# The first norm of a four-layer kernel: two batches ahead of the attention, six inside it

## The chip, the core and the metric

The kernel runs on one core of a Trainium2 chip. The core has five engines with queues of their own: TensorE (PE in the profile; its weight loads are PEld), VectorE (DVE), ScalarE (ACT), GpSimd (POOL) and SyncE (SP), which here only issues DMA transfers. SBUF is the working memory with 128 partitions, PSUM the eight banks into which PE writes. The metric is the device time of one execution in microseconds (us): the median of three runs.

## The reference

Four layers work on x of 8 batches x 512 tokens x 128 features, in float32. Each one is a norm, an attention-like part s, a feed-forward part g, and a gated sum:

```python
xn = _layernorm(x, axis=-1)
s = _L0_attn_ref(xn, ...)          # 16 heads of 8, sliding window of 64
g = _silu(_L0_ffn_ref(xn, ...))    # six 128x128 weights in 4 bits with scales and low-rank parts
x = x + s * g
# layer 1: a recurrence over time (s) and experts, two of eight per token (g)
# layer 2: windowed and latent attention (s), a complex product (g)
# layer 3: complex attention with decays per head (s), soft experts (g)
```

The norm takes each token's mean and variance over the 128 features: `(x - m) / sqrt(v + eps)`. The change touches this first norm, layer 0's attention, and work that prepares weights for later layers:

- decoding in layer 0: `w = q / 7.5 - 1`, times a scale per group of 16;
- mixing in layer 1: the key, value and receptance weights are scaled per input channel by the time mix, and by one minus it; the output weights are halved;
- scalars in layer 3: softplus, sigmoid, and a chain of products and reciprocals on 16 heads.

## The kernel before

x lies in SBUF with features on the partitions and tokens along the free axis. A batch is 512 tokens, and the norm's blocks are 512 tokens too (NTB is 8), so a block of the norm is a batch.

**Who orders the instructions.** Instructions issued through `in_order` (line 74) keep the order in which they are written, on each engine. All of them appear under line 83 in the profile, so they are told apart by the names of their tiles. Other instructions are placed by a scheduler, each as early as its operands and its buffers let it. A pool of buffers hands one out again when its last reader is done; the profile shows that as a wait on that reader.

**The start** (`network`, line 2757). SP loads x in eight parts, then the weights of layers 2 and 1 (in the constructors of `L2Consts` and `L1Consts`), then the attention's `a0_w` and `a0_b`, then layer 0's 4-bit weights (`l0_load`). The norm runs over all eight blocks. Then `l0_decode`, `l2.fill` and `l1.fill` are written (masks and counters on POOL; two large loads m1_w13 and m1_w2 from ACT's queue; the mixing on ACT), and then the attention. `l3_scalars` is written after layer 0, but it is left to the scheduler, and the profile shows it between 34 and 43 us.

**The norm** (`layer_norm`, line 117). Four steps per block: `centre` (four PE products with the centring matrix into ps_c), `spread` (ACT squares, DVE sums to var, POOL takes the power -0.5 to rstd), `scale` (DVE multiplies ps_c by rstd into row), `turn` and `keep` (four PE transposes into ps_t, ACT copies to xn). It has all eight banks of PSUM; the attention's pools open when it ends.

**The attention** (`l0_attention`, line 225). It works in 64 units u, eight per batch; a unit is 128 tokens and eight heads. Three pools of PSUM: scores (two tiles of two banks), one bank of weighted sums, and three banks `p_t` for everything else. The loop writes, for unit u:

- `turned(u)`: eight PE transposes of the exponentials, in two halves (tp), each copied by ACT (pt);
- in even units `norm(u - 1)`: DVE takes the reciprocal (rec) and the product (o);
- `scores(u + 3)`: four PE products (sc), DVE adds the mask (e) and takes the maxima (mx), POOL subtracts them;
- in even units `out_rows`: one PE transpose (tpo), ACT adds a bias (ot);
- ACT's exponential of unit u + 2;
- `weigh(u)`: 16 small PE products (av; 32 records in the profile);
- in a batch's second unit `finish`: the output projection of the batch before (ps_o on PE, s on DVE);
- one step of `project`, for the next batch: first the key projection ps_k with the first two of four masked copies kb (DVE, then ACT), next the other two kb (DVE, then ACT), then the queries (ps_q), then the values in two parts (ps_v).

So the bank of ps_k is held from the end of a batch's first unit to the end of its second. From the fifth batch on, `l0_low_rank` adds a step in each batch's seventh unit, on the decoded weights. Behind the attention comes `l0_ffn`, which needs the decoded weights; layer 1 needs the mixing, and layer 3 the scalars.

Of the kernel before, what the change touches and what calls it, by code (L numbers as in the profile page):

```python
# [9 lines left out]
F32 = mybir.dt.float32  # L10
# [6 lines left out]
P = 128  # L17
# [10 lines left out]
class Net:  # L28
# [88 lines left out]
    def layer_norm(self, x, xn, gamma=None, beta=None, banks=(5, 3), free=False):  # L117
# [7 lines left out]
        with tc.tile_pool(name="ln_s", bufs=3) as sp, tc.tile_pool(  # L125
# [41 lines left out]
            for t in range(NTB + 3):  # L167
                if t < NTB:
                    centre(t)
                    spread(t)  # L170
                if 2 <= t < NTB + 2:
                    scale(t - 2)
                if t >= 3:
                    turn(t - 3)
                    keep(t - 3)
# [49 lines left out]
def l0_attention(net, xn, s_out, p0, w, bias):  # L225
# [6 lines left out]
    with ExitStack() as st:  # L232
# [148 lines left out]
        act.activation(e[1], e[1], AF.Exp)  # L381
        todo = iter(())
        for u in range(N + 2):
            if u < N and u % U == 0 and u // U + 1 < B:
                todo = project(u // U + 1)
# [20 lines left out]
            if u > 4 * U and u % U == 6:  # L406
                next(low, None)

# [290 lines left out]
class L1Consts:  # L699
    E = 8  # L700

    def __init__(self, net, st):
        nc, tc, E = net.nc, net.tc, self.E
        self.net = net
        self.p1 = p1 = st.enter_context(tc.tile_pool(name="a1_c", bufs=1))
# [7 lines left out]
    def fill(self):  # L713
        net, nc, p1, E = self.net, self.net.nc, self.p1, self.E
        act = net.in_order(nc.scalar)
        self.w13 = net.load(p1, "m1_w13", act)
        self.w2 = net.load(p1, "m1_w2", act)

        w, par = self.w, self.par
        self.td = td = p1.tile([P, 1], F32, tag="td", name="td")  # L720
        act.activation(td, par[:, 0:1], AF.Exp)
        act.activation(td, td, AF.Copy, scale=-1.0)
        self.tf = par[:, 1:2]
        self.wm = wm = p1.tile([P, 3, 2, P], F32, tag="wm", name="wm")
        self.rest = rest = p1.tile([P, 3], F32, tag="rest", name="rest")
        act.activation(rest, par[:, 2:5], AF.Identity, scale=-1.0, bias=net.ones[:, 0:1])
        for i in range(3):
            act.activation(wm[:, i, 0, :], w[:, i, :], AF.Copy, scale=par[:, 2 + i : 3 + i])
            act.activation(wm[:, i, 1, :], w[:, i, :], AF.Copy, scale=rest[:, i : i + 1])
        act.activation(w[:, 3, :], w[:, 3, :], AF.Copy, scale=0.5)  # L730
# [22 lines left out]
        nc.gpsimd.memset(self.keep[:, :, 0:1], 0.0)  # L753

# [554 lines left out]
class L2Consts:  # L1309
# [4 lines left out]
    def __init__(self, net, st):  # L1314
# [5 lines left out]
        self.p1 = p1 = st.enter_context(tc.tile_pool(name="a2_c", bufs=1))  # L1320
# [1315 lines left out]
class Prepared:  # L2636
# [29 lines left out]
    def l0_decode(self):  # L2666
        nc, wt, qw, sc = self.net.nc, self.f0_wt, self.qw, self.sc
        nc.vector.tensor_copy(wt, qw)
        nc.vector.tensor_scalar(wt, wt, 1.0 / 7.5, -1.0, ALU.mult, ALU.add)
        nc.vector.tensor_tensor(wt, wt, sc, ALU.mult)  # L2670
# [34 lines left out]
    def l3_scalars(self):  # L2705
# [9 lines left out]
        nc.vector.scalar_tensor_tensor(sp, raw, -1.0, raw, ALU.mult, ALU.min)  # L2715
        nc.scalar.activation(sp, sp, AF.Exp)
        nc.scalar.activation(sp, sp, AF.Ln, bias=net.ones[:, 0:1])
        nc.vector.scalar_tensor_tensor(sp, raw, 0.0, sp, ALU.max, ALU.add)
        sig2, eta2, gam2, nu = (sp[:, i, :] for i in range(4))

# [4 lines left out]
        nc.scalar.activation(mu, par[:, 0, :], AF.Exp, scale=-1.0)  # L2725
        nc.vector.tensor_scalar(mu, mu, 1.0, None, ALU.add)
        nc.vector.reciprocal(mu, mu)
        nc.vector.tensor_scalar(mu, mu, 1e-4, None, ALU.add)
        nc.vector.tensor_scalar(nmu, mu, -1.0, None, ALU.mult)

        nc.vector.tensor_scalar(v_e2, nmu, 2.0, None, ALU.mult)
        nc.vector.reciprocal(v_e2, v_e2)
# [132 lines left out]
```

## Time and profile before

| What | us |
|---|---|
| Median of three runs | 2364.72 (2363.43 to 2366.03) |
| The profiled execution's own time | 2379.87 |
| Its span, first to last instruction | 2378.2 |
| First scores of the attention | 43.24 |
| First transposes of the attention | 50.97 |
| Key projections (ps_k) of the next batches | 56.59, 101.52, 133.36, 165.21, 197.05, 229.61, 262.38 |

Over the whole span PE is busy 93%, DVE 84%, ACT 78%, POOL 66%. The profile cuts the span into 40 slices of 59.5 us; the first five hold all that the change moves. A digit is the busy share in tenths, PEclk is the clock granted to TensorE in tenths of full speed:

```profile
PE   5999998989976999878999999999999999999888
DVE  4577778875675999759999999999999999999656
ACT  3566655555533899947999999999999999999865
POOL 4344435254264788656688888888788878887545
PEclk7799988999997999988999999999999999999999
```

A line of a timeline gives start and length in us, engine, line, operation, output and inputs, the number of instructions, and in brackets the idle time before it with what ended it. A line of a window gives the stretch, its length, and for each engine its busy time with the number of instructions in brackets; then the granted clock as a fraction of full speed, the DMA engines' share and GB/s. PE's busy time is that of records whose ends are modelled; a PE that is busy at clock 0.5 does half the work. A float32 product appears as two records, a transpose as one.

### The profile page before, as it was taken

Reading aid. Unit: us, or ns where it says so; the run is one execution under the profiler, and the core shown is the slowest. Engines: PE = TensorE matmul, PEld = TensorE weight load, DVE = VectorE, ACT = ScalarE, POOL = GpSimd, SP = SyncE. Lnnn points to the kernel's source line nnn. Section 1 sums busy time; section 2 is a strip of 40 time slices with the busy share of each in tenths; the row PEclk is TensorE's granted clock in tenths of the full one; section 3 lists DMA queues with packets and bytes.
Section 4 is the critical chain, followed back from the end, with each engine's and each line's share of the span. In section 5 each row is a group of like instructions: output and inputs, shape, how many; then the busy total and the mean of one; then the engine's idle time right before and its main releaser. Section 6 shows DMA issues by size and latency. Waiting matters only on the chain.

```text
span 2378.2 us, 48959 instructions
## 1 busy us (share of the span) xinstructions
PE 2203.3 (93%) x17762; PEld 1535.1 (65%) x17762; DVE 1996.1 (84%) x3579; ACT 1854.9 (78%) x3906; POOL 1575.0 (66%) x1414
## 2 busy tenths in 40 slices
PE   5999998989976999878999999999999999999888
PEld 4666676656533666645767777777777777777676
DVE  4577778875675999759999999999999999999656
ACT  3566655555533899947999999999999999999865
POOL 4344435254264788656688888888788878887545
PEclk7799988999997999988999999999999999999999
DMA  4000001012210000043334344443444344433100
GB/s 141 2 2 2 2 1 36 9 50 66 46 43 20 3 16 16 29 119 98 99 98 116 103 105 103 104 104 103 109 106 109 91 109 114 107 97 85 41 1 37
DMA packets 91617, 156.94 MB, mean 66 GB/s; under 512 B 20144, under 2 KB 44464, under 8 KB 91120
## 3 DMA queue, kind: packets, MB, share of 16 engines
q1 hardware_dynamic: 86736, 140.95, 22.7%
q0 software_dynamic: 4352, 8.92, 1.6%
q10 hardware_dynamic: 288, 3.93, 0.4%
q8 instruction: 142, 2.33, 0.4%
q14 instruction: 99, 0.81, 0.1%
HBM read 30.52 MB, written 12.06 MB: 18 GB/s over the span
## 4 chain that ended last, share of the span: by engine, by line
PE 58%; DVE 28%; issue 4%; POOL 4%; ACT 4%; DMA 1%; SPq 1%; another core or an unknown queue 0%; DVEq 0%; ACTq 0%; POOLq 0%
PE sc L83 11%; DVE sc L83 8%; DVE y L83 6%; DVE r L83 6%; PE ps_av L83 6%; PE tp L83 5%; PE ps_u L83 5%; PE ps_kq L83 5%; PE ps_n L83 3%; PE av L83 3%; PE ps_ab L83 3%; PE ps_v L83 2%; DVE mx L83 2%; DVE e L83 2%; PE ps_y L83 1%
## 5 line engine op out<-in xcount | busy, mean ns | idle before, releaser
L83 POOL TENSOR_TENSOR ek<-E,kn 128x512 f32<-128x512 f32 (+3 forms) x512 | 433.5, 868 | 209.6 <-DMA kn<-nr 205.9
L83 POOL TENSOR_TENSOR e<-e,mx 128x1024 f32<-128x1024 f32 x112 | 212.1, 1899 | 190.1 <-DVE mx L83 93.6
L83 PE MATMUL sc<-r 128*128 128x512 f32 (+3 forms) x1024 | 311.9, 448 | 26.9 <-DVE y L83 24.0
L83 POOL TENSOR_TENSOR r<-r,rs 128x1024 f32<-128x1024 f32 x128 | 303.8, 2373 | 22.9 <-DMA rs<-r 17.7
L83 PE MATMUL ps_av<-u,at 128*128 128x128 f32 x2560 | 308.1, 276 | 0.8 <-ACT o L83 0.8
L83 PEld LDWEIGHTS ps_av<-u,at 128*128 128x128 f32 x2560 | 297.4, 193 | 1.1 <-ACT o L83 1.1
L83 ACT ACTIVATE y<-y,mn 128x384 f32<-128x384 f32 (+3 forms) x512 | 288.4, 569 | 4.0 <-DVE mn L83 3.2
L83 PEld LDWEIGHTS sc<-r 128*128 128x128 f32 x1024 | 166.2, 192 | 192.6 <-issue 125.6
L83 DVE SCALAR_TENSOR_TENSOR y<-sc,qn,V 128x512 f32<-128x512 f32 (+3 forms) x512 | 246.6, 544 | 9.1 <-DVE sc L83 0.5
L83 DVE CUSTOM_DVE_ANT_0 y<-y,ps_g,ncs 128x384 f32<-128x384 f32 (+3 forms) x512 | 253.1, 540 | 0.0
L83 PEld LDWEIGHTS tp<-ident,y 128*128 128x128 f32 x1280 | 161.4, 141 | 115.3 <-issue 48.7
L83 ACT ACT_TABLE_LOAD x179 | 229.7, 1283 | 3.9 <-PEq L2854 0.8
L83 PE MATMUL tp<-ident,y 128*128 128x128 f32 x1280 | 203.7, 274 | 3.4 <-ACT o L83 1.4
L83 ACT COPY at<-tp 128x512 f32<-128x512 f32 (+1 forms) x384 | 195.1, 508 | 7.6 <-PE tp L83 4.6
L83 DVE SCALAR_TENSOR_TENSOR sc<-sc,ek 128x1280 f32<-128x1280 f32 x128 | 189.6, 1482 | 8.9 <-issue 3.8
L83 DVE TENSOR_TENSOR sc<-sc,EF 128x1280 f32<-128x1280 f32 x128 | 191.9, 1499 | 4.4
L83 POOL TENSOR_TENSOR s<-s,o 128x512 f32<-128x512 f32 x120 | 153.7, 1281 | 32.5 <-ACT o L83 32.5
L83 ACT ACTIVATE y<-y 128x1280 f32<-128x1280 f32 x128 | 163.4, 1277 | 6.5 <-DVE y L83 5.8
L83 DVE TENSOR_TENSOR r<-sn,ps_kq 128x1024 f32<-128x1024 f32 x128 | 155.1, 1212 | 10.3 <-ACT sq L83 5.4
L83 ACT ACTIVATE sq<-ps_kq 128x1024 f32<-128x1024 f32 x128 | 131.5, 1027 | 33.6 <-PE ps_kq L83 33.6
L83 DVE TENSOR_TENSOR r<-ct,ps_kq 128x1024 f32<-128x1024 f32 x128 | 155.0, 1211 | 0.0
L83 ACT ACTIVATE e<-e 128x1024 f32<-128x1024 f32 x112 | 117.3, 1061 | 40.5 <-POOL e L83 40.0
(459 smaller groups left out, 5035.7 us busy)
## 6 DMA issues: line engine op xcount, KB each, us to landing
rs<-r SPq DMA_DIRECT2D x256, 256.0 KB
kn<-nr SPq DMA_DIRECT2D x512, 64.0 KB
yrows<-yy SPq DMA_DIRECT2D x36, 128.0 KB
ct<-trig SPq DMA_DIRECT2D x16, 256.0 KB
EF<-E SPq DMA_DIRECT2D x16, 256.0 KB
EF<-E SPq DMA_DIRECT2D x16, 192.0 KB
m_w<-m_w ACTq DMA_DIRECT2D x1, 2560.0 KB
x<-x SPq DMA_DIRECT2D x8, 256.0 KB
```

Source lines behind the costliest of these rows:

```text
L83: ins = op(*args, **kwargs)
```

## The change

`layer_norm` gets a number of blocks, and `network` asks for two. The other six blocks become steps in the attention's loop: a generator `centred(b)` for the block two batches ahead. It is advanced at the top of a batch's second to seventh unit, ahead of the unit's transposes: the products and a copy to SBUF by ACT (lc), the square on ACT, the sum on DVE, the power and the product on POOL, an empty step, then the transposes into a `p_t` bank and the copy to xn.

A second chain, `early()`, is advanced at the top of the fourth, sixth and eighth unit from the second batch on: decoding (three steps, its last product on POOL instead of DVE), mixing (six steps on ACT), and the scalars of layer 3 (on DVE and ACT, in written order now).

The loads of layers 2 and 1 move out of the constructors into `load()`, called behind `l0_load`; so the attention's weights are the first load after x. The two large loads of `l1.fill` move from ACT's queue to SP's.

```diff
-    def layer_norm(self, x, xn, gamma=None, beta=None, banks=(5, 3), free=False):
+    def layer_norm(self, x, xn, gamma=None, beta=None, banks=(5, 3), free=False, n=NTB):
...
-            for t in range(NTB + 3):
-                if t < NTB:
+            for t in range(n + 3):
+                if t < n:
...
-def l0_attention(net, xn, s_out, p0, w, bias):
+def l0_attention(net, x, xn, s_out, p0, w, bias, l1):
...
+        def centred(b):
+            ps = p_t.tile([P, 4, P], F32, tag="t", name="ps_c")
+            for k in range(4):
+                pe.matmul(
+                    ps[:, k, :], lhsT=x[:, ts(4 * b + k, P)], rhs=net.cmat,
+                    start=True, stop=True,
+                )
+            c = p2.tile([P, 4, P], F32, tag="lc", name="lc")
+            act.copy(c, ps)
+            yield
+            sq = p2.tile([P, 4, P], F32, tag="sq", name="sq")
+            act.activation(sq, c, AF.Square, scale=net.inv_root)
+            var = p2.tile([P, 4], F32, tag="var", name="var")
+            std = p2.tile([P, 4], F32, tag="rstd", name="rstd")
+            yield
+            dve.tensor_reduce(var, sq, AX.X, ALU.add)
+            dve.tensor_scalar(var, var, EPS, None, ALU.add)
+            yield
+            pool.tensor_tensor(std, var, net.neg_half.to_broadcast([P, 4]), ALU.pow)
+            pool.tensor_tensor(c, c, std.unsqueeze(2).to_broadcast([P, 4, P]), ALU.mult)
+            yield
+            yield
+            ps = p_t.tile([P, 4, P], F32, tag="t", name="ps_t")
+            for k in range(4):
+                pe.transpose(ps[:, k, :], c[:, k, :], net.ident)
+            act.copy(xn[:, ts(b, S)], ps.rearrange("p k q -> p (k q)"))
+            yield
+
+        def early():
+            yield from net.prep.l0_decode(dve, pool)
+            yield from l1.mixing(act)
+            yield from net.prep.l3_scalars(dve, act)
+
+        rest = early()
         todo = iter(())
+        norms = iter(())
         for u in range(N + 2):
+            if u % U == 0 and u // U + 2 < B:
+                norms = centred(u // U + 2)
+            if 0 < u % U < 7:
+                next(norms, None)
+            if u >= U and u % U in (3, 5, 7):
+                next(rest, None)
...
-        act = net.in_order(nc.scalar)
-        self.w13 = net.load(p1, "m1_w13", act)
-        self.w2 = net.load(p1, "m1_w2", act)
+        self.w13 = net.load(p1, "m1_w13")
+        self.w2 = net.load(p1, "m1_w2")
...
+    def mixing(self, act):
+        act.activation(td, par[:, 0:1], AF.Exp)
+        act.activation(td, td, AF.Copy, scale=-1.0)
+        yield
+        act.activation(rest, par[:, 2:5], AF.Identity, scale=-1.0, bias=net.ones[:, 0:1])
+        yield
+        for i in range(3):
+            act.activation(wm[:, i, 0, :], w[:, i, :], AF.Copy, scale=par[:, 2 + i : 3 + i])
+            act.activation(wm[:, i, 1, :], w[:, i, :], AF.Copy, scale=rest[:, i : i + 1])
+            yield
+        act.activation(w[:, 3, :], w[:, 3, :], AF.Copy, scale=0.5)
+        yield
...
-        nc.vector.tensor_tensor(wt, wt, sc, ALU.mult)
+        yield
+        pool.tensor_tensor(wt, wt, sc, ALU.mult)
+        yield
...
-    def l3_scalars(self):
+    def l3_scalars(self, dve, act):
...
+        yield
+        dve.scalar_tensor_tensor(sp, raw, -1.0, raw, ALU.mult, ALU.min)
+        act.activation(sp, sp, AF.Exp)
+        act.activation(mu, par[:, 0, :], AF.Exp, scale=-1.0)
+        yield
+        act.activation(sp, sp, AF.Ln, bias=net.ones[:, 0:1])
+        yield
...
-            net.layer_norm(x, xn)
-            prep.l0_decode()
+            l2.load()
+            l1.load()
+            net.layer_norm(x, xn, n=2)
             l2.fill()
             l1.fill()
-            l0_attention(net, xn, s, p0, w0, b0)
+            l0_attention(net, x, xn, s, p0, w0, b0, l1)
             l0_ffn(net, x, xn, s, l1)
-        prep.l3_scalars()
```

## The prediction

> **What bounds the kernel now.** I read the page first (the chain that ended last, then the 40 slices), then stage windows of the first 395 us, then the timeline of 0 to 60 us and of one batch in the middle of the attention. Everything that the change touches lies before 310 us of the 2378.2 us span, so only that stretch is priced. Its windows (time stretch, length, then busy time and count of PE, PEld, DVE, ACT and POOL, granted clock, DMA share, GB/s):
>
> ```profile
> 0.00:43.24 43.24, 23.21 (x115) 19.36 (x115) 18.57 (x54) 18.85 (x36) 22.07 (x73) 0.79 0.60 194
> 56.59:101.52 44.93, 44.43 (x409) 29.02 (x407) 22.60 (x27) 20.08 (x32) 15.08 (x8) 0.63 0.00 1
> 133.36:165.21 31.85, 30.51 (x409) 19.97 (x409) 23.55 (x28) 20.79 (x33) 15.17 (x9) 1.00 0.01 2
> ```
>
> The reader is to see three stages. Up to 43.24, where the first scores start, no engine is busy much over half of the time: this is a chain of waits. From there a batch of the attention is the stretch from one key projection (ps_k) to the next. In steady state it takes 31.85 us with PE busy 30.51 of it: PE is the bound, and DVE (23.55), ACT (20.79) and POOL (15.17) have room. The first such batch holds the same 409 PE records and takes 44.93 us at a mean clock of 0.63, which is 13.1 us more. Finer windows put the clock at 0.50 without a break from 48.6 to 89.6, though PE is busy nearly all of that time.
>
> The start, from the timeline (start, length, engine, operation):
>
> ```profile
> 10.88 4.00 POOL L83 TENSOR_TENSOR rstd<-var,neg_half 128x4 f32<-128x4 f32 x4
> 30.55 2.07 PE L83 MATMUL ps_k<-xn,a_w 128*128 128x512 f32 x2 [0.67 <-ACT xn L83]
> 36.99 0.76 ACT L83 ACTIVATE kb<-ps_k,kbias,hm 128x512 f32<-128x512 f32 x1
> ...
> 40.84 0.76 ACT L83 ACTIVATE kb<-ps_k,kbias,hm 128x512 f32<-128x512 f32 x1
> 43.24 2.01 PE L83 MATMUL sc<-kb,q 32*64 32x512 f32 x16
> ```
>
> The first projection waits for the last of eight norm blocks (30.55). Then ACT's part of the keys (kb), which is ready to run at about 33.5, runs at 36.99 and 40.84, because mixing weights and the scalars of the last layer, with two table loads, stand before and between.
>
> **The change part by part.** The program order of the changed kernel was compared with the old one on each engine.
>
> *Norm cut to two blocks; decoding, mixing and scalars taken out of the start.* POOL still runs the constants first (the same 8.2 us of memsets and selects, ending at 10.9), so the first inverse root stays at 10.88. Each takes 1.0 us; so the second row product starts at 12.95 (0.69 us), its four transposes take 0.66 to 1.12 us (both clocks are in the old timeline) and the copy to xn 0.58: done at 15.0 to 15.6. The projection weights were the thirteenth load after x (issued at 12.58) and become the first; the load that has this place now is issued at 4.53 and lands 6.24 us later, at 10.8, so they are no wait. So ps_k starts at about 15.3 instead of 30.55. From there: ps_k 2.07, then four kb halves that run one after the other, DVE 0.81, ACT 0.76, DVE 0.81, ACT 0.76 with 0.1 us between them (3.4), then six ps_v records (1.65) that need the bank of ps_k: 15.3 + 2.07 + 3.4 + 1.65 = 22.4 for the first scores instead of 43.24. Bounds: 21.5 with the projections at full clock, 23.5 if a small load is late. **Term: -20.9 us.** POOL's masks and value memsets (29.99 to 35.49 now, right behind the norm) follow the norm at about 15 and end at 20.5; the first subtraction needs POOL at 27, so they are covered.
>
> *Moved loads.* The two large expert weights (1.60 us of ACT issue at 29.92) go to SP's queue behind the small loads. On SP the load of the scalars' parameters is queued behind them; its first reader now comes at unit 37 (over 150 us later), and the next SP work is the row store at about 395 us. The layer 1 and 2 loads move behind those of layer 0 and are read after 400 us. Nothing, in either direction.
>
> *Six norm blocks inside the attention, two batches ahead.* Per block PE gets 8 ps_c records (1.06 us at full clock at 13.20 us) and 4 transposes (half of tp's 1.04): 1.6 us, the lower end, since PE is the bound. The upper end comes from what waits. This is the place, a batch's first and second unit after the projection:
>
> ```profile
> 165.14 1.12 PE L83 MATMUL ps_k<-xn,a_w 128*128 128x512 f32 x2
> 166.10 1.04 PE L83 MATMUL tp<-ident,e 128*128 128x128 f32 x8
> 167.15 0.78 ACT L83 ACTIVATE kb<-ps_k,kbias,hm 128x512 f32<-128x512 f32 x1 [0.76 <-DVE kb L83]
> 167.82 1.06 ACT L83 COPY pt<-tp 128x512 f32<-128x512 f32 x2
> 168.45 1.12 PE L83 MATMUL av<-vw,pt 128*64 128x9 f32 x32 [0.30 <-ACT pt L83]
> ...
> 171.55 0.66 PE L83 MATMUL tp<-ident,e 128*128 128x128 f32 x4 [0.48 <-DVE s L83]
> ...
> 172.25 0.78 ACT L83 ACTIVATE kb<-ps_k,kbias,hm 128x512 f32<-128x512 f32 x1 [2.41 <-DVE kb L83]
> 172.93 1.06 ACT L83 COPY pt<-tp 128x512 f32<-128x512 f32 x2
> 173.56 1.12 PE L83 MATMUL av<-vw,pt 128*64 128x9 f32 x32
> ```
>
> Unit one: ps_k keeps one of the three transpose banks over this unit, ps_c takes the second, so the second half of tp needs the bank of ps_c, which ACT's copy (lc, 0.58 like the xn copies) frees only after kb: 167.9 + 0.58 = 168.5. Then 0.55 of tp, 1.05 of scores, and av starts at 170.1 instead of 168.45: +1.65. Unit two: kb slides to 174.2, the square (0.60) follows it before pt, and av starts at 176.1 instead of 173.56: +2.5 so far. Unit six: transposes 0.55, less the 0.25 for which the output transpose waits for DVE there: +0.3 to +0.55. The sum (0.86 of DVE in unit three) falls into DVE's 1.85 us of idle time before that unit's scores. The root and product of unit four (1.0, and 0.95 to 1.28 by half of the 128x1024 subtraction's 1.90 and by the 128x512 product's 1.28) fall into POOL's 2.2 idle us, to within 0.3. So 2.95 per block, between 1.6 and 3.8. Five blocks lie in full-clock batches. **Term: 5 x 2.95 = +14.75 us.**
>
> *The clock in the first batch.* The clock changes of the start (17.9, 24.7, 28.1, 34.9, 38.4, 45.2, 48.6, 89.6) are all multiples of 3.41 us apart, as if counted in such windows. Windows that led to a rise held 128-wide products throughout (31.6 to 35.0, projections), or a projection and transposes with some scores (86.2 to 89.6); windows with much of av (64-wide weights, 9 columns) did not. In the changed order, ps_k (2.0 at half clock), ps_c (2.1) and tp (1.7) stand in a row, 5.8 us, from 5.6 us after the first transposes. That covers most of a window wherever the windows fall, so I expect the rise within 9 to 12 us of the first transposes, against 38.6 now. At the second unit's transposes (64.03) the changed kernel is then level with the old one, ps_c paid by the clock; the rest of the batch takes the old kernel 101.5 - 64.0 = 37.5 us, the new one 26.5 (the steady stretch from 170.47 to 196.98) plus 0.6 and 0.4 of norm steps less 1.2 (no output projection in this unit yet) = 26.3. **Term: -11.2 us**; bounds 0 (no earlier rise; then the block also costs 4 at half clock) and -13.1.
>
> The Trainium skill has a rule on this: "TensorE: Matmul & The Clock Gate", part 1, says that the gate opens after about 3.4 us of sustained busy time. The step of 3.41 us agrees with the rows, but 37 busy us at 0.50 (from 52 to 89.6) do not. By the page's rule alone the old kernel would have had nothing to gain here and the sum would be about -3.4.
>
> *The rest as steps.* The logarithm's two table loads (2 x 1.28) and 0.35 come into a unit seven, where ACT's exp ends at 191.54 and pt starts at once: pt slides by 1.65, the next exp is reloaded behind it, and the next unit's pt arrives only just in time: +1.6 (0 to 2.9). Mixing: two of 0.39 ahead of pt, in unit seven +0.55, in units three and five 0.1 to 0.2: 0.9 in all. Exponentials 0.3. Decoding (0.56 and 0.55 on DVE, the product, 0.95 on DVE now, on POOL at 1.3 to 1.9) and the 22 small DVE operations (0.11 to 0.25 each) fall into 1.0 to 1.9 us of DVE idle time before the scores of odd units; without that cover they would cost 4 more. **Term: +2.8 us** (1 to 6).
>
> **Sum:** -20.9 + 14.75 - 11.2 + 2.8 = -14.5 us against the profiled execution's 2379.87 (span 2378.2), that is -0.61%. The timed median is 2364.72, 15.2 less; the same share of it gives **2350.3 us**. What can be told from no change is about 0.2%, 4.7 us.
>
> **The rivals.**
>
> *A. The early rise brings nothing in the timed runs.* Either those runs already rise earlier than the profiled one (the 15.2 us between them would allow it), or the change does not bring it forward. For: one execution shows 0.50 for 41 us, and nothing shows what the others had. Against: three times within 2.6 us of each other. Then -20.9 + 14.75 + 2.8 and 0 to 4 for the first block: -3.4 to +0.7, near 2363.
>
> *B. The half clock lasts longer, into the second batch: slower.* Place: after the first ps_k. Price: 13.1 us per batch at half clock. If two batches run so, -20.9 + 4 + 4 x 2.95 + 13.1 + 2.8 + 3 (second block at half clock) = +14, near 2379. It decides for slower once the rise comes some 14 us later than the 38.6 of now (0.29 us per us, from +0.7). For: the old kernel let three runs of 3.7 us (projection and transposes) pass without a rise. Against: the run is now 5.8 us.
>
> *C. The norm steps cost PE time only.* If PE has another order of bank releases than I read, 1.6 per block: 5 x 1.35 less, -21, near 2344. For: PE's waits on ACT in a steady batch are 0.3 us in all. Against: the second half of tp does wait for ACT at that place in the changed order.
>
> **How the numbers follow.** Main case 0.53 (-9 to -20), A 0.20, B 0.13, C 0.14. Faster: main and C and a quarter of A, 0.71; within 0.2%: most of A, 0.15; slower: B and a bit, 0.14. The range leaves out B: from 2341 (C with the start at its lower bound) to 2366 (the upper end of A).
>
> **What would show it.** Right: first scores near 22; the clock at 1.00 before 45; 34.8 us from ps_k to ps_k in batches two to six, with the second half of tp waiting for ACT's lc; one longer unit with two table loads near 170; the norm blocks' sums and roots in no wait. Wrong: the clock at 0.50 beyond 60, batches over 37 us, or a first projection that waits for a load.

## The result, and the profile after

| | Before | Changed |
|---|---|---|
| Median | 2365.38 us (4 runs, 2363.43 to 2370.01) | 2396.66 us (4 runs, 2375.44 to 2403.02) |
| Profiled execution's own time, span | 2379.87, 2378.2 | 2391.97, 2390.3 |

The ratio is 1.0117, 95% interval 1.0086 to 1.0148: the changed kernel is slower, by about 28 us (31 between the medians), where 14 us faster was forecast. The four runs of the changed kernel spread over 28 us, and their mean granted clocks nearly go with it: 2375.44 at 0.964, 2391.97 (the profiled one) at 0.954, 2403.02 at 0.950, 2401.35 at 0.948. One run of the changed kernel in a later comparison (`after_again`, 2388.01 us) was in the slow state: it counts in that median, and is left out of the ratio and the means.

The windows of the changed kernel, in the columns of those before: the start up to the first scores, then batches from ps_k to ps_k (the last of them, the seventh, to the ps_o behind it).

```profile
0.00:21.86 21.86, 11.43 (x42) 8.10 (x42) 6.10 (x11) 6.11 (x9) 15.32 (x67) 1.00 0.68 190
34.33:76.04 41.71, 39.61 (x420) 26.74 (x418) 24.49 (x29) 21.75 (x35) 17.00 (x10) 0.77 0.01 2
76.04:119.96 43.92, 41.35 (x425) 27.56 (x421) 26.55 (x32) 22.63 (x36) 18.80 (x12) 0.77 0.00 1
119.96:156.07 36.11, 33.64 (x424) 22.33 (x420) 25.52 (x29) 23.36 (x41) 17.47 (x11) 0.95 0.00 1
156.07:190.70 34.63, 31.96 (x425) 21.34 (x421) 25.63 (x31) 23.56 (x41) 17.18 (x11) 1.00 0.01 2
228.91:267.81 38.90, 34.28 (x428) 22.82 (x424) 30.89 (x47) 22.29 (x36) 16.95 (x10) 0.96 0.01 1
267.81:314.88 47.07, 44.41 (x465) 28.50 (x461) 30.84 (x43) 24.35 (x37) 17.30 (x10) 0.76 0.01 2
```

The start is as forecast: scores at 21.86 instead of 43.24. The fourth batch, the only one at full clock throughout, is as forecast too: 34.63 us, against 31.85. But before, batches two to seven all ran at 1.00; now the second runs at 0.77, the third at 0.95, the fifth at 0.91, the sixth at 0.96 and the seventh at 0.76. The clock did rise early; it did not stay. Windows of 3.41 us, laid so that the changes of the clock fall on their edges, show both behind the second ps_k, and a later fall in the second batch:

```profile
36.32:39.73 3.41, 3.41 (x17) 2.96 (x15) 0.81 (x1) 1.95 (x3) 0.78 (x1) 0.50 0.00 0
39.73:43.14 3.41, 3.41 (x53) 2.28 (x56) 2.02 (x2) 1.54 (x2) 0.00 (x0) 1.00 0.00 0
43.14:46.55 3.41, 1.55 (x23) 0.55 (x15) 3.27 (x6) 2.23 (x5) 1.90 (x1) 1.00 0.00 0
46.55:49.96 3.41, 3.41 (x28) 2.25 (x27) 2.73 (x3) 1.42 (x4) 1.90 (x1) 0.50 0.02 5
84.09:87.50 3.41, 2.48 (x31) 1.31 (x33) 2.68 (x5) 2.37 (x5) 1.69 (x1) 1.00 0.00 0
87.50:90.91 3.41, 3.41 (x26) 2.25 (x23) 3.38 (x4) 1.50 (x3) 1.90 (x1) 0.50 0.00 0
```

The clock rises at 39.73. In the window ahead of the first fall (46.55) PE is busy for 1.55 us of 3.41, and ahead of the other (87.50) for 2.48. The timeline ahead of the second (in brackets the idle time before and what ended it):

```profile
79.36 0.66 PE L83 MATMUL tp<-ident,e 128*128 128x128 f32 x4 [0.86 <-ACT lc L83]
...
84.43 0.66 PE L83 MATMUL tp<-ident,e 128*128 128x128 f32 x4 [0.87 <-DVE s L83]
...
86.95 1.51 PE L83 MATMUL av<-vw,pt 128*64 128x9 f32 x32 [0.59 <-ACT pt L83]
...
88.39 2.08 PE L83 MATMUL ps_q<-xn,a_w 128*128 128x512 f32 x2
```

Three waits of 0.6 to 0.9 us within 8 us, all in the two units where the norm block's first steps stand (lc ahead of pt on ACT, then kb later, then the square). The weighted sums behind them take 1.51 (1.13 in a full-clock batch) and the next projection 2.08 instead of 1.12: the clock has halved. What PE waited for from 60 to 330 us (us in total, times, longest):

```profile
PE tpo L83 <- DVE o L83: 4.8, 7, 1.7
PE tp L83 <- ACT lc L83: 4.6, 5, 1.1
PE av L83 <- ACT pt L83: 4.5, 7, 1.1
PE tp L83 <- DVE s L83: 4.4, 5, 0.9
```

And in the kernel before, from 60 to 310 us:

```profile
PE tpo L83 <- DVE o L83: 4.2, 15, 0.5
PE tp L83 <- DVE s L83: 2.9, 6, 0.5
PE av L83 <- ACT pt L83: 1.8, 6, 0.3
```

The waits are not many more. They are longer: no wait of these groups lasted over 0.5 us before; now the longest of each is 0.9 to 1.7.

That is one execution. The changed kernel was profiled twice more, as `after_again` and `after_third`, on two chips. In both the first batch takes 34.97 us at 0.94. In `after_third`, the batch and then two windows in it, at the place of the first fall above:

```profile
34.41:69.38 34.97, 32.73 (x420) 22.26 (x419) 24.50 (x29) 21.42 (x35) 17.01 (x10) 0.94 0.01 2
41.75:45.17 3.42, 2.20 (x17) 0.96 (x15) 3.28 (x6) 1.19 (x2) 1.77 (x1) 1.00 0.00 0
45.17:48.58 3.41, 2.77 (x41) 2.23 (x42) 3.27 (x4) 2.84 (x6) 1.65 (x2) 1.00 0.02 5
```

PE is busy for only 2.20 us of 3.42, less than the 2.48 ahead of the fall at 87.50, and the clock stays. From the second ps_k to the last ps_o these two executions take 292.60 and 281.00 us at mean clocks of 0.90 and 0.94, where the first took 307.88 at 0.85. The longest waits of `after_third` are the same (1.7 us for o, 1.1 for pt). So how much half clock the waits bring differs from execution to execution.

**The sum by stages**, for the first profile of each kernel. Half-clock time below is 2 x (1 - granted clock) x length. Up to the second ps_k: 34.33 against 56.59, -22.3 us. From there to the last ps_o: 307.88 against 266.31, +41.6. In that stretch half-clock time summed over the batches' windows is 92.5 us, against 44.6. The old first batch gives a price: 13.1 us lost for 33.2 us of half clock, 0.39 us per us. So 47.9 x 0.39 = 18.7 of the 41.6 are clock, and 22.9 is time that would be there at full clock. By the same price the other two executions of the changed kernel give 20.0 and 19.6 for it. At the row store the changed kernel is 19.0 behind (412.47 against 393.51), at the end 12.1; what gave back 6.9 in the later layers stays open.

### The profile page after: what moved, and what is told of

Same layout as the page of the kernel before. It is cut to its first block, busy times and chain, and to the rows that moved or that the text cites. A ratio compares the mean times of both kernels' runs of the same rounds, so it can differ in the third digit from the quotient of the medians.

```text
span 2390.3 us, 48946 instructions
## 1 busy us (share of the span) xinstructions
PE 2214.8 (93%) x17762; PEld 1543.5 (65%) x17762; DVE 2003.6 (84%) x3572; ACT 1858.0 (78%) x3912; POOL 1582.3 (66%) x1421
## 4 chain that ended last, share of the span: by engine, by line
PE 56%; DVE 29%; POOL 4%; ACT 4%; issue 4%; DMA 1%; SPq 1%; another core or an unknown queue 1%; DVEq 0%; POOLq 0%; ACTq 0%
PE sc L83 10%; DVE sc L83 8%; DVE y L83 6%; DVE r L83 6%; PE ps_av L83 6%; PE tp L83 5%; PE ps_u L83 4%; PE ps_kq L83 4%; PE ps_n L83 3%; PE ps_ab L83 3%; PE av L83 2%; DVE mx L83 2%; PE ps_v L83 2%; DVE e L83 2%; PE ps_y L83 1%
## 5 line engine op out<-in xcount | busy, mean ns | idle before, releaser
L83 DVE TENSOR_TENSOR r<-sn,ps_kq 128x1024 f32<-128x1024 f32 x128 | 155.3, 1213 | 10.8 <-PE ps_vo L2066 5.4
L83 DVE SCALAR_TENSOR_TENSOR e<-sc,maskFalse 128x1024 f32<-128x1024 f32 (+1 forms) x96 | 90.4, 952 | 76.4 <-PE sc L83 73.4
```

The costliest lines, as they stand in the source:

```text
L83: ins = op(*args, **kwargs)
```

## The experiments

The theories. **G**: a stretch of some 3.4 us in which PE waits for ACT or DVE lets the clock fall, and the steps in the loop make such stretches. **W**: the added work itself is the loss. **S**: the small steps of mixing and scalars make the falls, not the norm. Later **C** (the loss comes with the chip), **F** (unused products help any kernel) and **D** (any shift of the loop against the start upsets the clock) joined.

The kernels ran in five comparisons, each on one chip beside the kernel before. "More half clock" is the mean over a kernel's runs, from each run's span and mean granted clock, less that of the kernel before. Within a kernel the span follows the half-clock time from run to run (correlation 0.90 to 0.95), with a slope of 0.44, 0.39, 0.39, 0.38 and 0.36 us per us in the five; the last two columns split the difference of mean spans by it.

| Before, us | Kernel | Median, us | Ratio to before | More half clock, us | by the clock, us | the rest, us |
|---|---|---|---|---|---|---|
| 2364.62 | e1_shift | 2376.28 | 1.0050 [1.0022, 1.0077] | +33.7 | +14.8 | -0.7 |
| | e2_rest_only | 2374.92 | 1.0046 [1.0021, 1.0071] | +32.7 | +14.3 | -3.0 |
| | e3_norm_only | 2385.93 | 1.0094 [1.0057, 1.0131] | +30.9 | +13.5 | +4.8 |
| | e4_fill | 2369.76 | 1.0029 [1.0006, 1.0052] | +8.9 | +3.9 | +2.0 |
| 2343.66 | after_again | 2353.78 | 1.0058 [1.0030, 1.0086] | +16.9 | +6.7 | +6.4 |
| | e5_before_fill | 2342.40 | 0.9993 [0.9975, 1.0011] | -10.2 | -4.0 | +3.2 |
| | e6_before_wait | 2374.39 | 1.0104 [1.0065, 1.0142] | +45.7 | +18.0 | +8.5 |
| | e7_shift_late | 2337.33 | 0.9975 [0.9955, 0.9995] | -14.3 | -5.6 | +0.9 |
| 2368.72 | e7_again | 2370.94 | 1.0001 [0.9978, 1.0023] | -3.2 | -1.3 | +1.4 |
| | e3_again | 2382.37 | 1.0055 [1.0028, 1.0083] | +20.3 | +7.9 | +4.2 |
| | e9_best | 2377.63 | 1.0051 [1.0025, 1.0076] | +8.7 | +3.4 | +6.9 |
| | e8_before_fill3 | 2369.95 | 1.0015 [0.9993, 1.0037] | -6.6 | -2.6 | +4.6 |
| 2344.20 | after_third | 2361.85 | 1.0083 [1.0067, 1.0098] | +24.0 | +9.1 | +6.1 |
| | e4_again | 2355.95 | 1.0047 [1.0029, 1.0064] | +13.8 | +5.2 | +6.8 |
| | e7_third | 2340.59 | 0.9989 [0.9972, 1.0007] | -7.0 | -2.7 | +1.2 |
| | e10_ahead_late | 2332.02 | 0.9948 [0.9933, 0.9963] | -28.7 | -10.9 | -0.9 |
| 2364.53 | e2_again | 2375.92 | 1.0030 [1.0004, 1.0055] | +22.4 | +8.0 | -1.0 |
| | e10_again | 2353.21 | 0.9959 [0.9939, 0.9978] | -19.5 | -7.0 | -3.1 |

The ratio and its 95% interval need not agree with the medians to the last digit. The split gives all half clock one price; that of the start, where no engine is the bound, should cost less, which was not measured. Before has 18.2 us of it ahead of the first scores in its profile, the change 0 to 10: its "rest" of +6 therefore holds some 3 to 7 us of loop clock (8 to 18 us at 0.38, an estimate).

### Do short waits alone bring the half clock?

To the kernel before, two unused ACT copies per batch are added where the change has lc and sq. PE gets no work.

```diff
                     act.activation(kb[b][:, c, :], ps, AF.Identity, scale=hm, bias=hb)
+                    if b > 0:
+                        idle = p2.tile([P, S], F32, tag="idle", name="idle")
+                        act.copy(idle, q[b - 1])
                     yield
```

> The old kernel with one unused copy on ACT (about 0.55 us) behind each of ACT's two kb copies of a batch, where the change has lc and sq: PE gets no work, only waits in the second and third unit. Theory G: the waits alone cost 7 x 1.1 = 8 us, and the lighter stretches drop the clock more often, 20 to 50 us more at half clock, so 2380 to 2395. Rival W (the work on PE is the cause): 2364 to 2373.

Measured: 1.0104, nearly what the whole change cost in its first comparison, and more than its 1.0058 on this chip (6 runs, interval 1.0065 to 1.0142). The wait for pt in the first unit of the second and third batch, with the copies:

```profile
98.32 1.32 PE L83 MATMUL av<-vw,pt 128*64 128x9 f32 x32 [0.82 <-ACT pt L83]
99.57 2.08 PE L83 MATMUL ps_o<-ot,a_w 128*128 128x512 f32 x2
...
133.90 1.13 PE L83 MATMUL av<-vw,pt 128*64 128x9 f32 x32 [0.81 <-ACT pt L83]
```

The same place in the kernel before:

```profile
104.76 1.13 PE L83 MATMUL av<-vw,pt 128*64 128x9 f32 x32 [0.30 <-ACT pt L83]
...
136.60 1.13 PE L83 MATMUL av<-vw,pt 128*64 128x9 f32 x32 [0.30 <-ACT pt L83]
```

A wait of 0.30 becomes 0.82, and right behind the first of them a projection takes 2.08 instead of 1.12; behind the second, just as long, the clock stays. From 54 to 330 us the profile has 8.4 us of waits for pt (13 times) where the kernel before has 2.5 (7 times): 5.9 us more, the greater part of the rest of 8.5. The other 18.0 is half clock. Windows of this kernel: the 3.41 us ahead of that fall and behind it, then the second to fourth batch, all three at 1.00 in the kernel before:

```profile
95.68:99.09 3.41, 2.59 (x42) 1.54 (x40) 2.13 (x3) 2.65 (x6) 1.90 (x1) 1.00 0.00 0
99.09:102.50 3.41, 3.41 (x20) 1.85 (x17) 1.92 (x3) 0.62 (x1) 1.89 (x1) 0.50 0.00 0
94.48:130.07 35.59, 33.70 (x413) 21.77 (x409) 23.66 (x28) 21.93 (x35) 15.18 (x9) 0.90 0.01 2
130.07:164.48 34.41, 32.11 (x412) 20.96 (x409) 23.64 (x28) 21.83 (x35) 15.16 (x9) 0.95 0.01 2
164.48:203.61 39.13, 36.83 (x413) 24.05 (x409) 23.65 (x28) 22.00 (x35) 15.17 (x9) 0.83 0.01 1
```

Ahead of the fall PE is busy for 2.59 us of 3.41. A window around the same place in the kernel before, with no fall behind it:

```profile
103.00:106.41 3.41, 3.11 (x47) 1.80 (x45) 2.13 (x3) 2.70 (x4) 1.69 (x1) 1.00 0.00 0
```

So the core of G is shown: waits of half a microsecond, with the same PE work, cost more through the clock than by themselves. That any such stretch lets the clock fall is not: `after_third` passed one with 2.20 us busy. The Trainium skill, "TensorE: Matmul & The Clock Gate", part 1, "A second HAM failure mode: psum-queue depth-cycling", tells of a kernel whose short idle gaps between groups of products make the clock swing between half and full. That agrees with these rows (0.82 idle, clock 0.90 over the batch). The part's first table names an idle window of about 3.4 us for the fall; the falls looked at came behind windows with PE busy for 1.55, 2.48 and 2.59 us of 3.41.

### What does the place of the norm steps do?

`e1_shift` is the change with the norm's steps two units later, behind both pairs of kb (units four to eight, and the first unit of the next batch).

```diff
+            if u % U == 0 or u % U > 2:
+                next(norms, None)
             if u % U == 0 and u // U + 2 < B:
                 norms = centred(u // U + 2)
-            if 0 < u % U < 7:
-                next(norms, None)
```

`e3_norm_only` keeps the place of the norm steps and puts mixing and scalars behind the loop; decoding stays in it. `e7_shift_late` is both.

```diff
         def early():
             yield from net.prep.l0_decode(dve, pool)
-            yield from l1.mixing(act)
-            yield from net.prep.l3_scalars(dve, act)
...
-        for _ in rest:
+        for _ in l1.mixing(act):
+            pass
+        for _ in net.prep.l3_scalars(dve, act):
             pass
```

> The changed kernel with the six norm blocks' steps moved by two units: they stand in a batch's fourth to eighth unit and the first of the next, behind the key projection, instead of the second to seventh. The work is the same. Theory G (the granted clock: PE's waits for ACT and DVE in the second and third unit leave a light stretch of about 3.4 us, and the clock falls to half after it): those waits are as in the old kernel, the clock stays at 1.00 in the steady batches outside the unit with the table loads, a batch takes about 33.5 us, time 2345 to 2360. Rival W (the added work itself, wherever it stands): 2385 to 2400 as in the changed kernel. Rival S (the small steps of mixing and scalars cause the falls): the falls near 222 and 297 us stay, 2372 to 2385.

> The changed kernel with mixing and scalars behind the attention's loop (about 10 us of ACT and DVE work there, partly beside PE); decoding and the six norm blocks in the loop as in the change. Theory G: the second half of tp still waits for ACT's copy, the clock still falls in the second to sixth batch, none near 222 and 297; 2378 to 2398. Rival W: 2385 to 2400. Rival S: no falls, 2355 to 2368.

> The changed kernel, unchanged, in as many runs as the experiments, to stand beside them. All theories: 2385 to 2400, with about 220 us of the span's clock time at half (the span times twice one minus the mean granted clock), against about 170 in the old kernel.

> The norm blocks' steps moved by two units as in the shifted kernel, and mixing and scalars behind the attention's loop. Theory G with both causes (the light third unit, and units in which ACT and DVE steps of mixing and scalars hold PE up): the shifted kernel's falls at units with scalars go, half-clock time 150 to 180 us, 2355 to 2368. Rival (the small steps do nothing): as the shifted kernel or a few us more, 2376 to 2384.

Each of the two edits alone still left 31 to 34 us more half clock on the first chip. For e1_shift that is a miss of G (2345 to 2360 expected, 2376.28 measured, in S's range); e3_norm_only lies in G's range and in W's, not in S's. The change itself came out far below the 2385 to 2400 and the 220 us of half clock that all theories expected on the second chip (2353.78 and 177 us). Both edits together, on that chip, took the half clock below the kernel before (-14.3), and the kernel was a little faster (0.9975), where the change itself was 1.0058; on two more chips it was level with the kernel before (1.0001 and 0.9989). Its batches two to four, windows:

```profile
71.17:105.43 34.26, 31.95 (x424) 21.38 (x420) 26.37 (x32) 21.83 (x36) 18.55 (x11) 1.00 0.01 1
105.43:139.21 33.78, 31.95 (x425) 21.38 (x421) 25.42 (x30) 22.54 (x37) 17.61 (x11) 1.00 0.01 1
139.21:172.99 33.78, 31.95 (x425) 21.36 (x421) 25.26 (x29) 22.18 (x37) 17.13 (x10) 1.00 0.01 2
```

PE is busy for the same 31.95 as in the change's full-clock batch, but the batch takes 33.78 instead of 34.63: a block costs 1.9 us here instead of 2.8, since PE waits 0.85 less. The change's batch holds mixing steps too; in a batch of `e3_again`, which holds none, a block costs 2.6 (35.20 against 32.56 us, its fifth batch). To set the chip aside, the pair was run side by side.

> The variant with the norm steps two units later and the mixing and scalars behind the loop, once more, beside the three that follow. G (the loss is half clock after light stretches): 0.9975 as on the chip before, +-0.003; under 165 us of half clock in the profile. W (the work itself): the six blocks cost the same here as in the change, so 1.000 or more. C (the chip decides: the loss comes and goes with the chip, not with the place of the steps): the ratio lands by the others, within 0.003 of the variant with the norm steps unmoved.

> The same, but with the norm steps where the change has them; mixing and scalars behind the loop. Beside the run before this tells what the place of the norm steps alone is worth on one chip. G: the light stretches of the first two units stay, so 15 to 25 us slower than with the steps moved, 190 to 220 us of half clock. W: as with the steps moved, within 5 us. C: as with the steps moved, within 7 us.

> The changed kernel beside the three variants that follow, on one chip. G (the loss is half clock after light stretches; norm steps and the steps of mixing and scalars both make them): 1.006 to 1.012, 20 to 50 us more half clock than the kernel before, and 10 to 25 us above the variant with moved steps. C (the loss comes and goes with the chip): within 5 us of the variant with moved steps.

> The variant with the norm steps two units later and mixing and scalars behind the loop, beside the change. G: 0.998 to 1.001 of the kernel before, and 10 to 25 us faster than the change, of which 60 to 90 per cent by less half clock. W: 3 to 7 us faster than the change, for the steps taken out of the loop alone.

On one chip, moving the norm steps two units was worth 11.4 us of median (e3_again to e7_again): 23.5 us less half clock, 9.2 us at 0.39, and 2.8 in the rest. That is less than G's 15 to 25, and more than W or C allow. The profiled e7_again had 170.6 us of half clock, not under 165. Beside the change itself, on another chip, e7_third was 21.3 us faster; of the 16.7 us between the mean spans 31.0 us of half clock are 11.8 (71%), as G had it. C falls as an account of the sign: the change was slower in all three comparisons, by 0.6 to 1.2%. That its size differs by a factor of two stays unexplained.

### What do mixing and scalars do in the loop?

`e2_rest_only` has all eight norm blocks ahead of the attention, as before; decoding, mixing and scalars are steps in the loop, and the attention's weights come first. `e10_ahead_late` is the same with mixing and scalars behind the loop (the edit above).

```diff
-            net.layer_norm(x, xn, n=2)
+            net.layer_norm(x, xn)
...
-            if u % U == 0 and u // U + 2 < B:
-                norms = centred(u // U + 2)
-            if 0 < u % U < 7:
-                next(norms, None)
```

> The changed kernel with all eight norm blocks ahead of the attention again; loads first, decoding, mixing and scalars as steps in the loop as in the change. Theory G: first scores near 37.5 instead of 43.2, no light second or third unit, clock as in the old kernel except around the table loads, time 2358 to 2368. Rival W: the same, 2358 to 2368. Rival S: falls of the clock at the steps, 2372 to 2385.

> All eight blocks of the norm ahead of the attention, as before; the attention's weights loaded first, decoding as steps in the loop, mixing and scalars behind it. So the start loses only what stood in ACT's and DVE's way there (6.2 us at the first projection, as in the variant that left the steps in the loop). G: the loop is nearly that of the kernel before, so half clock is within 10 us of its, and the time 3 to 7 us below it (0.997 to 0.9987). Rival D (any shift of the loop against the start changes where the clock falls, and upsets it): 20 to 35 us more half clock, 4 to 10 us slower than before.

> All eight norm blocks ahead, decoding, mixing and scalars as steps in the loop, beside the same kernel with mixing and scalars behind the loop. S (the steps of mixing and scalars in the loop bring half clock by themselves): 1.003 to 1.006 of the kernel before, 25 to 45 us more half clock than the variant with them behind the loop. C (it was the chip): within 0.002 of the variant beside it.

> All eight norm blocks ahead, decoding in the loop, mixing and scalars behind it, on another run. S and G: 0.993 to 0.998 of the kernel before, half clock less than before's. C: 0.998 or more.

With mixing and scalars in the loop: slower than before twice, with 22 to 33 us more half clock. With them behind it: 0.9948 and 0.9959, the fastest of all. Side by side the two differ by 22.7 us of median and 41.9 us of half clock, inside the 25 to 45 that S and G expected. G alone had expected only as much half clock as before (within 10 us); 28.7 and 19.5 less were measured, and D's 20 to 35 more did not come. The windows of e2_again, its third to sixth batch:

```profile
117.61:149.51 31.90, 30.55 (x412) 19.98 (x409) 23.37 (x27) 21.76 (x38) 15.25 (x9) 1.00 0.01 2
149.51:183.17 33.66, 32.19 (x413) 20.89 (x409) 23.75 (x29) 22.07 (x38) 15.12 (x9) 0.95 0.01 2
183.17:218.59 35.42, 33.35 (x418) 21.71 (x414) 24.32 (x29) 25.29 (x40) 15.34 (x9) 0.93 0.01 2
218.59:261.29 42.70, 41.03 (x414) 25.82 (x412) 28.99 (x44) 21.12 (x33) 15.18 (x8) 0.74 0.01 2
```

And of e10_again, its first, fourth, fifth and sixth:

```profile
42.31:76.77 34.46, 32.62 (x409) 21.61 (x407) 22.45 (x27) 19.79 (x32) 15.02 (x8) 0.90 0.01 2
...
140.47:172.32 31.85, 30.50 (x412) 19.96 (x408) 23.56 (x28) 20.82 (x33) 15.18 (x9) 1.00 0.01 2
172.32:204.89 32.57, 31.23 (x419) 20.68 (x415) 23.57 (x28) 21.32 (x34) 14.88 (x9) 1.00 0.01 2
204.89:237.65 32.76, 31.16 (x416) 20.48 (x413) 25.48 (x32) 21.04 (x33) 15.42 (x9) 1.00 0.01 2
```

The sixth batch holds twelve more DVE operations than its twin (44 against 32), small ones, and takes 42.70 us at 0.74 instead of 32.76 at 1.00. So S's mechanism holds, but not its "not the norm": e3, which has no such steps, brings half clock too. Why the first batch, where the two programs do not differ yet, runs at 0.90 here and at 0.72 in e2_again's profile (42.04 us) is not settled; the changes of the clock stand at other offsets from the start in the two (1.3 and 2.2 us on a grid of 3.41).

e10 also takes the start apart. Its second ps_k is at 42.31, against 56.59 before and 34.33 in the change: of the change's 22.3 us at the start, 14.3 came from decoding, mixing, scalars and load order, and only 8.0 from the six norm blocks. In e10_ahead_late's profile it is at 45.08, with more half clock ahead of it (0.84 instead of 1.00 up to the first scores), so 11.5 and 10.8 by that one. Behind the loop mixing and scalars cost 4.1: from the last ps_o to the row store 74.73 us, against 70.61.

### Do unused products hold the clock up?

Three products whose results nothing reads, in each batch's third unit; in the change (`e4_fill`), in e7 (`e9_best`, with four more, once, behind the first projection of the loop), in the kernel before (`e8_before_fill3`, on xn). `e5_before_fill` is the kernel before with the four alone.

```diff
+            if u % U == 1:
+                for k in range(1, 4):
+                    pe.matmul(
+                        tp[:, k, :], lhsT=x[:, ts(k, P)], rhs=net.cmat, start=True, stop=True
+                    )
             pe.transpose(tp[:, 0, :], o.rearrange("p h d -> p (h d)"), net.ident)
```

> The changed kernel with three more 128-wide products on PE in the third unit of each batch, ahead of the output transpose, into unused columns of its tile; their results are not used. PE gets 8 x 0.8 = 6.4 us more work at full clock. Theory G: the added products lift the light stretch, the clock stays at 1.00 in most steady batches, and the time falls in spite of the work, to 2362 to 2380. Rivals W and S: 2400 to 2410, the changed kernel plus 6.

> The changed kernel with three unused products in each batch's third unit. G: they cost 0 to 7 us of PE time and shorten the half clock by 20 to 45 us, so 3 to 15 us faster than the change beside it. W (PE's work is what counts): 0 to 7 us slower than the change beside it. The same products did not shorten it in the variant with moved steps, so if they do nothing here either, the earlier reading of them, taken against a run of the change on another chip, falls.

> Norm steps two units later, mixing and scalars behind the loop, and unused 128-wide products: four behind the first projection of the loop, three ahead of the output transpose in each batch's third unit (their results are read by nothing). The products cost PE up to 0.8 us per batch and 1 us once, 7.5 us in all, if PE is the bound there. G: half clock falls by 10 to 25 us, at 0.41 us each 4 to 10 less, so between 6 us faster and 3 us slower than without the products. W: 7 us slower than without them.

> The kernel before with the three unused products in each batch's third unit alone. G: the kernel before has few light stretches in its steady batches, so there is little to win back: half clock stays at 150 to 170 us, and the time is 0 to 7 us above the kernel before. F (unused products help any kernel, wherever it stands): 5 to 25 us faster, as they were worth in the changed kernel.

> The old kernel with four more 128-wide products on PE, once, behind the first key projection of the loop; their results are not used. This is the place where the change has its first ps_c. Theory G (a stretch of dense products of more than 3.4 us lifts the clock, a light one drops it): the clock rises within 12 us of the first transposes in nearly all runs, 10 to 25 us less at half clock, time 4 to 10 us less, 2353 to 2362. Rival: the first batch's half clock does not depend on that, 2364 to 2367.

e4_fill looked like a proof of G: 27 us faster than the change. But the two had not run in one comparison. Side by side (e4_again) the products were worth 5.9 us of median, 3.2 of the mean spans and 10.2 us of half clock, not the 20 to 45 expected; with 10 runs over 15 us against 6 over 24 that is not clear of the noise. In e9 they brought 12 us more half clock, and 6.7 us of time, W's figure. In the kernel before they changed nothing that can be told, in line with G and against F; the four at the start (e5) neither, where G had expected 4 to 10 us. So filling is no cure that these runs show: in the change a small help is not shown, in e7 it did harm.

The kept traces say more on which products count for the clock. Laid on its own grid of 3.41 us, the 20 profiles have 1211 windows at full clock between 60 and 310 us, and behind 110 of them the clock falls. PE's busy time tells only part of it: it falls behind 57 of the 133 windows with PE busy below 80%, and behind 9 of the 926 with 90% or more. Weighed by kind it is nearly sharp. Count each record of a transpose or of a product of 128 columns with 0.13 us, of one of 512 columns with 0.56, of scores with half of their 0.13, of weighted sums with nothing: the clock falls behind all 58 windows with less than 1.2 us in all, and behind none of the 965 with 1.6 or more. At half clock it rises behind 96 of the 100 windows with 1.6 or more and behind none of the 124 below 1.4. These weights were chosen on the same windows, and no run tests them. By them a wait matters where it pushes projections and transposes out of a window.

## Why the prediction was wrong, point by point

- **The start, -20.9:** right. -22.3 up to the second ps_k; ps_k at 15.49 (15.3 forecast), first scores at 21.86 (22.4).
- **The norm blocks, 2.95 each:** right. 2.79 in the full-clock batch (2.6 without mixing steps in it), with the second half of tp waiting 0.86 for lc, as described.
- **The rest as steps, +2.8:** too low. At full clock the loop grew by 22.9 us (19.6 and 20.0 in the other two executions), where 14.75 + 2.8 and 1.0 for the first block were counted: 1 to 4 short. The logarithm's unit looks as forecast, at 222 instead of near 170. From the timeline:

```profile
222.35 1.28 ACT L83 ACT_TABLE_LOAD   x1
...
224.52 1.12 PE L83 MATMUL av<-vw,pt 128*64 128x9 f32 x32 [1.12 <-ACT pt L83]
...
224.97 1.28 ACT L83 ACT_TABLE_LOAD   x1
```

  The small DVE operations were costed at 0.11 to 0.25 each, under the cover of idle DVE time. One of a kind can take ten times that:

```profile
290.79 1.90 POOL L83 TENSOR_TENSOR e<-e,mx 128x1024 f32<-128x1024 f32 x1 [2.54 <-DVE cs L83]
290.95 1.77 DVE L83 TENSOR_TENSOR cs<-cs,coef 128x16 f32<-128x16 f32 x1
...
296.41 0.30 PE L83 MATMUL tpo<-ident,o 128*128 128x128 f32 x1 [1.71 <-DVE o L83]
```

  It took 0.11 in the kernel before; here it ends as POOL's subtraction ends. The output transposes 4 us later wait 1.71 for DVE, and at 299.1 the clock falls.
- **The clock in the first batch, -11.2: this is the step that failed.** The rise itself was right: 11.0 us after the first transposes (39.73), and 9.5 us after them in the other two executions, where 9 to 12 were forecast. But the step went on as if the clock, once up, stayed up ("the new one 26.5"), because the old kernel's did. It priced PE's new waits by their length alone and never asked what they do to the clock. In the first profile it fell at 46.55, the first batch gained 3.15 us of 11.2, and over the loop there were 47.9 us more half clock, +18.7 us. In the other two the first batch gained 9.9, near the forecast, and the clock fell in later batches. In the mean over the runs beside the kernel before, the change has 16.9 and 24.0 us more half clock, +6.7 and +9.1 us, where the step had -11.2 (29 us less half clock at the same price).
- **The base of that step.** It took one execution's first batch (33.2 us of half clock) for the kernel's. That execution has 199.8 us of half clock in all; the 137 runs of the old kernel beside the experiments have 160 to 173 in the mean of each chip, and only one of them more than 199.8. So a usual run had much less than 29 us to give, an estimate from these totals. That the difference lies in the first batch is likely, not shown: no other execution of the old kernel was profiled. In the kernels most like it the first batch took 39.52 us at 0.79 (e8_before_fill3) and 37.04 at 0.86 (e5_before_fill), not 44.93 at 0.63.
- **The rivals.** A: the early rise came, but its first condition, that the timed runs are better off than the profiled one, fits the 137 runs; its -3.4 to +0.7 lacks the half clock that the change brought. C: waits counted, not PE time alone. B had the right sign, by another way: its clock rose late, some 14 us later than the 38.6 of before; the real one rose 11 us after the first transposes, and fell again. Its half clock in the second batch is in the first profile (0.77), not in the other two (1.00). The signs named for "wrong" (half clock beyond 60, batches over 37 us) are what was seen.
- **What the sum could have told.** Split by cause, the norm's move had 8.0 to 10.8 us to gain at the start (e10's second ps_k against the change's) and 2.6 to 2.95 a block to pay, 16 to 18 for six. It was a loss at full clock already. The rest of the start's gain did not need it: e10 keeps 11.5 to 14.3, pays 4.1, and came out 11.3 and 12.2 us of median faster. One term for the whole start hid this.

## What to carry to other kernels

Where PE is the bound, price an added wait twice: by its length, and by the half clock that it may bring; here some 6 to 8 us of waits of 0.5 us each brought 18 us more, at 0.36 to 0.44 us per us of half clock. Before moving a chain of work under a tight loop, split the gain by what each part frees, and set each against its own cost in the loop: small preparations belong where no engine is late, even if they lie open there (4.1 us), and a clock seen in one execution, here the old kernel's first batch at half clock, is not a state to build a sum on. Compare variants only side by side on one chip: a reading of 27 us shrank to 6 or less when that was done.

## What the runs showed of the hardware that was not expected

- The clock falls behind stretches of 3.41 us in which PE is still busy for 1.55, 2.48 and 2.59 us, and stays behind others with 2.20. What divides them in these traces is how much of projections and transposes a stretch holds: below 1.2 us of them (scores at half) it fell behind 58 of 58, at 1.6 and more behind none of 965.
- Half clock costs less than half of its time: 0.36 to 0.44 us per us.
- The changes of the clock lie on a grid of 3.41 us in both kernels' profiled executions, but with another offset from the start (0.8 and 2.2 us). The same program shows 2375 to 2403 us. This fits a grid that runs free of the program; it wasn't tested by itself. Where two executions of one kernel happen on the same offset (0.7 us in after_again and after_third, on two chips), their first 17 changes of the clock, up to 267 us, agree to 0.1 us.
- DVE operations of 0.1 to 0.2 us take up to 1.8 beside a POOL instruction and end with it. The Trainium skill, "SBUF — State Buffer", section "SBUF: two separate sides", says of VectorE's and GpSimd's shared pair of ports that, for a VectorE operation with two inputs in SBUF against a GpSimd one that reads SBUF, whichever starts first holds it for the whole instruction while the other is blocked. That agrees with the 1.77 above (two inputs, cs and coef): POOL started at 290.79, 0.16 us earlier.
